# A state-space layer on one core: exp gets PSUM banks of its own, small products share one bank, transposes of a step share a two-bank tile

## Chip, cores, metric

One core of a Trainium2 chip runs the whole program in one launch. The metric is the device time in microseconds (us), the median of the runs; a profiled execution of its own gives the trace. TensorE is called PE, VectorE DVE, ScalarE ACT, GpSimd POOL and SyncE SP in the profile; PEld is PE's weight load.

## The reference, cut to what matters

The network has four residual layers, each `x = x + layer(group_norm(x))`, on x of shape (4, 64, 64, 128). The change touches layer 0 alone, a selective scan over an image in four directions:

```
xz = x @ in_proj.T;  xh, z = split(xz);  z = silu(z)
xc = silu(depthwise_conv3x3(xh) + conv_b)          # 256 channels, 64 x 64
xs = xc along rows, along columns, and both reversed   # 4 directions, L = 4096
x_dbl = einsum(xs, x_proj)                         # splits into dts (8), B (16), C (16)
delta = softplus(dt_proj @ dts + bias)
# per token t, channel d and state n (16 states):
h = exp(delta * A) * h + delta * u * B[n];   y = sum_n h[n] * C[n]
y = sum over the four directions of (y + D * xs), each put back in image order
out = (layer_norm(y) * z) @ out_proj.T
```

Layers 1 to 3 (a Fourier layer, a neural-operator layer, neighbourhood attention) are the same in both kernels.

## The kernel before, in words

**Units and steps.** Layer 0 is cut into 128 units: 4 images (batches), 4 directions in the order k = 1, 3, 0, 2, and 8 chunks of 512 tokens. A unit handles 256 channels as two halves s of 128 partitions. It has 16 steps n, one for each state; four steps make a group g, with q the place in the group. So there are 2048 steps.

**One step** (L405 to L424). POOL multiplies `du` by the broadcast row of B into `dB` (L413, both halves in one instruction). For each half ACT writes `dA = exp(delta * A)` into a PSUM bank (L420) and DVE scans 512 tokens, reading dA from PSUM, dB, and the state so far, into `h` (L421).

**Seven steps behind** (`LAG = 7`) PE turns h round so that the sum over states can be a matmul. `transpose` (L313) transposes four 128 x 128 blocks of h into one PSUM bank `pt` (L318), and ACT copies it to `hT` (L322); a step does this twice, so two banks of `pt` alternate. `products` (L341) multiplies a step's hT by `W` into `yT` (L363). W is C spread out: PE makes `cr` from `xd` (L433), DVE multiplies it by a diagonal mask (L436), four times a unit. After group 3, y is taken from yT (ACT L377 for k=1, else DVE adds at L379) and stored (L384); k=2 also takes statistics (L382).

**The next unit's inputs.** `fetch` (L264) loads u at n=3. `inputs` (L273) makes `xd_ps` on PE (L277) and copies it to `xd` on ACT (L279), writes B to a small DRAM scratch (L281), makes two `dp` on PE (L286), takes Exp twice and one Ln of both halves on ACT (L292, L293), clamps on DVE (L296), and forms `du` on POOL (L299). The scratch is one of three, `B{(8 * k + c) % 3}` (L280). Each group loads its rows of B with a broadcast to 128 partitions, `Bb` (L409), three buffers deep; before the change at the group's own first step.

**Neighbours' pieces.** `before(b)` (L139) is what image b needs ahead of its scan: group norm statistics (`gn_ps`, L148), normalisation (`x_ps` L172, `xn` L173), projection (`xh` L180, copied to `pad` L184), the convolution as nine matmuls a half into `cv` (L193), `zp` (L203), three Silus (L205, L208, L213) with an activation table load on each side, and stores. `after(b)` (L218) is what follows: layer norm (L236), transposes `pg` (L245), an affine copy (L246), the product with z on POOL (L250), `op` (L255), the residual addition (L260). Both are generators: image b+1's before() and image b-1's after() are spread as pieces over the steps of image b, one piece a step but for six values of n, until they are used up. The first image's before() runs ahead of the scans, and the last one's after() behind them.

**What sets the order.** Inside `tc.manual_schedule` (L389) PE, ACT, DVE and POOL run in the order in which the program emits (L386). SP, which issues the DMAs, is not among them: a planner orders its queue. A tile waits for a free buffer of its pool.

**PSUM** has eight banks: `l0ps` 2 (pt), `l0psx` 4, `l0psy` 2 (yT). The four of `l0psx` hold dA and every small product: cr, xd_ps, dp, cv, zp, and those of the pieces.

Of the kernel before, what the change touches and what calls it, by code (L numbers as in the profile page):

```python
# [16 lines left out]
P = 128  # L17
# [64 lines left out]
def layer0(sh, A, x_in, x_out, scr):  # L82
# [4 lines left out]

    tc, nc = sh.tc, sh.nc
    with ExitStack() as ctx:
# [4 lines left out]
        ps = pool("l0ps", 2, space=PSUM)  # L94
        psx = pool("l0psx", 4, space=PSUM)
# [43 lines left out]
        def before(b):  # L139

            st = small.tile([P, NCH, 6], F32, name="gn_st")
            for c in range(NCH):
                t = tmp.tile([P, 4, DM], F32, name="xs", tag="t2", bufs=4)
                nc.sync.dma_start(t, tiles(x_in(b)[c * CH : (c + 1) * CH, :]))
                yield 1
                pt = psx.tile([P, CH], F32, name="gn_ps", tag="x")
                for q in range(4):
                    nc.tensor.transpose(pt[:, q * P : (q + 1) * P], t[:, q, :], sh.ident)  # L148
                nc.vector.bn_stats(st[:, c, :], pt)
            yield 1  # L150
            s_, o_ = sh.group_scale(st, psx, small, "x")
            exp_and_ln()
            yield 1
            for c in range(NCH):
                r0, r1 = max(8 * c - 1, 0), min(8 * c + 9, 64)
# [11 lines left out]
                yield 1  # L167
                for j in range(0, j1 - j0, 3):
                    e = min(j + 3, j1 - j0)
                    pt = psx.tile([P, CH], F32, name="x_ps", tag="x")  # L170
                    for q in range(j, e):
                        nc.tensor.transpose(pt[:, (q - j) * P : (q - j + 1) * P], t[:, q, :], sh.ident)  # L172
                    nc.vector.tensor_scalar(xn[:, j * P : e * P], pt[:, 0 : (e - j) * P], s_, o_, ALU.mult, ALU.add)  # L173
                    yield 1
                for s in range(2):
                    for r in range(r0, r1, 5):
                        n = min(5, r1 - r)
                        pm = psx.tile([P, CH], F32, name="xh", tag="x")
                        o = (r - 2 * j0) * 64
                        nc.tensor.matmul(  # L180
                            pm[:, 0 : 64 * n], lhsT=w_in[:, s, :], rhs=xn[:, o : o + 64 * n], start=True, stop=True
                        )
                        p0 = r - 8 * c + 1
                        nc.scalar.copy(  # L184
                            pad[:, s, p0 : p0 + n, 1:65], pm[:, 0 : 64 * n].rearrange("p (h w) -> p h w", w=64)
                        )
                    yield 1
                o = (8 * c - 2 * j0) * 64
                for s in range(2):
                    pm = psx.tile([P, CH], F32, name="cv", tag="x")  # L190
                    for t in range(9):
                        dy, dx = divmod(t, 3)
# [7 lines left out]
                        if t < 8:  # L200
                            yield 1
# [14 lines left out]
                    yield 1  # L216

        def after(b, st):  # L218

            mv = small.tile([P, NJ, 2], F32, name="ln_mv")  # L220
            for j in range(NJ):
                nc.vector.bn_aggr(mv[:, j, :], st[:, j])
                if j % 8 == 7:
                    yield 1
            rs = sh.rstd(small, mv[:, :, 1], [P, NJ], "ln_r")
            exp_and_ln()
            for c in range(NCH):
                rows = slice(c * CH, (c + 1) * CH)
# [4 lines left out]
                yield 1  # L233
                for q in range(4):
                    j = 4 * c + q
# [3 lines left out]
                    if q % 2:  # L239
                        yield 1  # L240
                yg = tmp.tile([P, 2, CH], F32, name="yg", bufs=1)
                for s in range(2):
                    pt = psx.tile([P, CH], F32, name="pg", tag="x")
# [3 lines left out]
                    yield 1  # L247
# [3 lines left out]
                yield 1  # L251
                op = psx.tile([P, 4, DM], F32, name="op", tag="x")
                for q in range(4):
# [4 lines left out]
                    if q == 1:  # L258
                        yield 1
                nc.vector.tensor_tensor(xr, xr, op, ALU.add)  # L260
                nc.sync.dma_start(tiles(x_out(b)[rows, :]), xr)
                yield 1
# [10 lines left out]
        def inputs(k, c, u):  # L273

            xd_ps = psx.tile([40, CH], F32, name="xd_ps", tag="x")
# [6 lines left out]
            yield  # L282
            dps = []
            for s in range(2):
                dp = psx.tile([P, CH], F32, name="dp", tag="x")
                nc.tensor.matmul(dp, lhsT=w_dt[:, k, s * P : (s + 1) * P], rhs=xd, start=True, stop=True)  # L286
                dps.append(dp)
                yield
            delta = tmp.tile([P, 2, CH], F32, name="delta")

            for s in range(2):
                nc.scalar.activation(delta[:, s, :], dps[s], AF.Exp)  # L292
            nc.scalar.activation(delta, delta, AF.Ln, bias=1.0)  # L293
            yield
            for s in range(2):
                nc.vector.scalar_tensor_tensor(delta[:, s, :], delta[:, s, :], 88.0, dps[s], ALU.min, ALU.max)  # L296
            yield
            du = tmp.tile([P, 2, CH], F32, name="du")
            nc.gpsimd.tensor_tensor(du, delta, u, ALU.mult)  # L299
            yield xd, bd, delta, du  # L300

        for _ in before(0):
            pass
# [3 lines left out]
        for ready in inputs(*units[0][1:], v):  # L307
            pass
# [4 lines left out]
        def transpose(G, q, e):  # L313
            pt = ps.tile([P, 2, 2, P], F32, name="pt")
            for r in range(2):
                t0 = q * P + (2 * e + r) * 32
                for s in range(2):
                    nc.tensor.transpose(  # L318
                        pt[:, r, s, :], G["h"][:, s, t0 : t0 + 32, :].rearrange("p t n -> p (t n)"), sh.ident
                    )  # L320
            hT = tmp.tile([P, 2, 2 * P], F32, name="hT", bufs=4)
            nc.scalar.copy(hT, pt.rearrange("p r s d -> p r (s d)"))  # L322
            return hT

        def transposed(G):
# [3 lines left out]
            if G is not None:  # L329
                q = G["q"]  # L330
                G["q"] += 1
                hTs = [transpose(G, q, 0)]
                copied = G, q, hTs
            yield
            if todo is not None:
                products(*todo)
            if G is not None:
                hTs.append(transpose(G, q, 1))
            yield

        def products(G, q, hTs):  # L341
# [19 lines left out]
            for j in range(4):  # L361
# [4 lines left out]
                    rhs=hTs[j // 2][:, j % 2, :],  # L366
# [20 lines left out]
        pieces = []  # L387
        ends = {}
        with tc.manual_schedule(engines=order):  # L389
            for i, (b, k, c) in enumerate(units):  # L390
                if i % per == 0:
                    ln_st = small.tile([P, NJ, 1, 6], F32, name="ln_st")
                    if b + 1 < NB:
                        pieces.append(before(b + 1))
# [3 lines left out]
                xd, bd, delta, du = ready  # L398
# [5 lines left out]
                coming = None  # L404
                for n in range(NS):  # L405
                    g, q = divmod(n, 4)
                    if q == 0:
                        Bb = tmp.tile([P, 4, CH], F32, name="Bb", bufs=3)
                        nc.sync.dma_start(Bb, bd[4 * g : 4 * g + 4, :].partition_broadcast(P))  # L409
# [3 lines left out]
                    nc.gpsimd.tensor_tensor(dB, du, Bb[:, q : q + 1, :].to_broadcast([P, 2, CH]), ALU.mult)  # L413
                    behind = iter(())
                    if NS * i + n >= LAG:
                        H = queue[0]
                        behind = transposed(H)
                    for s in range(2):
# [5 lines left out]
                        next(behind, None)  # L424
# [3 lines left out]
                    if queue and queue[0]["q"] == 4:  # L428
                        queue.pop(0)
                    if n in (1, 5, 11, 13):  # L430
                        crg = (1, 5, 11, 13).index(n)
                        cr = psx.tile([P, CH], F32, name="cr", tag="x")
                        nc.tensor.matmul(cr, lhsT=sel[:, crg, :], rhs=xd[0:40, :], start=True, stop=True)  # L433
                    if n in (2, 6, 12, 14):
                        W = tmp.tile([P, 16, 32], F32, name="W", bufs=3)
                        nc.vector.tensor_tensor(  # L436
                            W,
                            cr.rearrange("p (a t) -> p a t", t=32),
                            diag[:, int(rev) : int(rev) + 1, :].to_broadcast([P, 16, 32]),
                            ALU.mult,  # L440
                        )
                        Ws[crg] = W
# [11 lines left out]
                    if i + 1 < len(units):  # L454
                        if n == 3:
                            u_next, v_next = fetch(*units[i + 1])
                        if n in (7, 8, 9):
                            coming = coming or inputs(*units[i + 1][1:], v_next)
                            next(coming)
                        if n in (10, 11):  # L460
# [13 lines left out]
                    if n not in (1, 5, 8, 9, 11, 13) and pieces:  # L474
                        if next(pieces[0], None) is None:
                            pieces.pop(0)
                if i + 1 < len(units):
                    u = u_next
                if i % per == per - 1:
                    for p in pieces:  # L480
                        for _ in p:
                            pass
                    pieces = []
                    pieces.append(late(after(b, ln_st)))
            while queue:
                for _ in transposed(queue[0]):
                    pass
                if queue[0]["q"] == 4:
                    queue.pop(0)
            for _ in transposed(None):  # L490
                pass
            for p in pieces:
                for _ in p:
                    pass


def late(pieces, n=8):

    for _ in range(n):
        yield 1  # L500
    yield from pieces
# [1214 lines left out]
```

## Time and profile before

| what | value |
|---|---|
| median of 3 runs | 9484.72 us (9472.2 to 9485.25) |
| the profiled execution, its own time | 9466.91 us |
| its span | 9465.1 us |
| mean granted TensorE clock | 0.889 |
| first scan to last scan of layer 0 | 218.6 to 6968.7 us |
| busy: PE, DVE, ACT, POOL | 7878.8, 7035.5, 6403.3, 5610.1 us |
| scans L421 | 4096, 4998.3 us |
| dB products L413 | 2048, 4829.1 us |
| exponentials L420 | 4096, 2864.3 us |
| copies L322 | 4096, 2416.9 us |

The profile comes from one execution. Busy time is a sum over stages with different limits, so it is read by stage. An idle time stands in front of an instruction and is put down to what ended it. A group's line gives the line of the kernel, engine, operation, tile written and tiles read, shapes and count, then busy time, mean of one in nanoseconds, idle time before it and what ended most of that.

### The profile page before, as it was taken

How to read it: one execution, taken by the hardware profiler on the slowest of the kernel's cores; microseconds unless marked ns; L12 is line 12 of the kernel's file. 1: busy time of each engine (PE TensorE's matmuls, PEld its weight loads, DVE VectorE, ACT ScalarE, POOL GpSimd, SP SyncE). 2: the span in 40 equal slices, each digit the busy share in tenths (PEclk: the TensorE clock that was granted, in tenths of full speed). 3: DMA queues.
4: the chain of work that ended last, by engine and by line, in shares of the span. 5: the costliest groups of instructions: out<-in, count | busy, mean ns of one | idle time of the engine just before them, and what ended most of it. 6: DMA issues, size and time to landing. Idle time of an engine off the chain costs nothing. (4 is left out here: it accounts for less than half of the span.)

```text
span 9465.1 us, 144952 instructions
## 1 busy us (share of the span) xinstructions
PE 7878.8 (83%) x54256; PEld 4499.6 (48%) x54256; DVE 7035.5 (74%) x8298; ACT 6403.3 (68%) x11773; POOL 5610.1 (59%) x2998
## 2 busy tenths in 40 slices
PE   7888888888888888888888888888869967677588
PEld 3444444444444444444444444444447756365366
DVE  1778788898887788888777898998954553443578
ACT  2878787777787777778777777888842211614467
POOL 1777778877777777777777878888840001010133
PEclk8989998888898998889999898999979988778699
DMA  6334443333444443334434333333332124131333
GB/s 112 110 115 127 115 128 123 113 121 128 125 126 118 117 122 115 136 121 119 118 118 126 110 137 123 130 128 114 131 116 53 35 59 132 51 103 50 88 87 86
DMA packets 1148677, 1038.13 MB, mean 110 GB/s; under 512 B 564127, under 2 KB 1001979, under 8 KB 1081156
## 3 DMA queue, kind: packets, MB, share of 16 engines
q1 hardware_dynamic: 1146292, 1027.13, 35.7%
q8 instruction: 426, 6.98, 0.3%
q14 instruction: 279, 2.29, 0.1%
q10 hardware_dynamic: 1680, 1.74, 0.1%
HBM read 845.18 MB, written 181.32 MB: 108 GB/s over the span
## 5 line engine op out<-in xcount | busy, mean ns | idle before, releaser
L421 DVE TENSOR_TENSOR_SCAN h<-dA,state,dB 128x512 f32<-128x512 f32 x4096 | 4998.3, 1271 | 1003.1 <-ACT dA L420 786.5
L413 POOL TENSOR_TENSOR dB<-du,Bb 128x1024 f32<-128x1024 f32 x2048 | 4829.1, 2374 | 1413.6 <-DVE h L421 1146.7
L420 ACT ACTIVATE dA<-delta,A_neg 128x512 f32<-128x512 f32 x4096 | 2864.3, 699 | 505.2 <-DVE h L421 428.5
L318 PEld LDWEIGHTS pt<-ident,h 128*128 128x128 f32 x16384 | 1948.6, 150 | 2008.3 <-issue 1303.5
L318 PE MATMUL pt<-ident,h 128*128 128x128 f32 x16384 | 2756.7, 299 | 103.8 <-ACT hT L322 103.8
L322 ACT COPY hT<-pt 128x512 f32<-128x512 f32 x4096 | 2416.9, 590 | 588.5 <-PE pt L318 552.9
L363 PE MATMUL yT<-hT,W 128*32 128x256 f32 x16384 | 1660.3, 418 | 18.0 <-ACT hT L322 15.2
L433 PE MATMUL cr<-xd,sel 40*128 40x512 f32 x1024 | 667.6, 736 | 460.5 <-DVE h L421 456.3
L363 PEld LDWEIGHTS yT<-hT,W 128*32 128x32 f32 x16384 | 409.7, 111 | 576.2 <-issue 374.0
L193 PE MATMUL cv<-pad,taps 128*128 128x512 f32 x1152 | 608.2, 629 | 0.0
L433 PEld LDWEIGHTS cr<-xd,sel 40*128 40x128 f32 x1024 | 169.4, 207 | 565.8 <-DVE h L421 514.4
L785 POOL TENSOR_TENSOR xg<-xg,so 128x1024 f32<-128x1024 f32 x8 | 26.6, 3343 | 693.4 <-ACT so L785 672.3
L1434 POOL TENSOR_TENSOR S<-S,sm 128x784 f32<-128x784 f32 x128 | 191.1, 1493 | 408.7 <-DVE sm L1432 348.4
L277 PE MATMUL xd_ps<-u,w_x 128*40 128x512 f32 x512 | 281.5, 678 | 134.2 <-DVE h L421 106.1
L286 PE MATMUL dp<-xd,w_dt 65*128 65x512 f32 x512 | 282.2, 634 | 113.6 <-DVE h L421 112.8
L299 POOL TENSOR_TENSOR du<-delta,u 128x1024 f32<-128x1024 f32 x128 | 304.0, 2375 | 66.3 <-DVE delta L296 66.3
L436 DVE TENSOR_TENSOR W<-cr,diag 128x512 f32<-128x512 f32 x512 | 341.4, 667 | 0.0
L785 POOL TENSOR_TENSOR z<-z,sp 128x1024 f32<-128x1024 f32 x16 | 41.8, 2616 | 465.4 <-ACT z L785 465.1
L1441 ACT ACTIVATE S<-S,mx 128x196 f32<-128x196 f32 x512 | 227.9, 448 | 33.9 <-DVE mx L1468 33.4
L785 PE MATMUL pz<-PT,WX 128*68 128x64 f32 x2048 | 167.1, 248 | 100.0 <-DVE WX L785 81.4
L193 PEld LDWEIGHTS cv<-pad,taps 128*128 128x128 f32 x1152 | 197.1, 203 | 106.1 <-issue 99.4
L279 ACT COPY xd<-xd_ps 40x512 f32<-40x512 f32 x128 | 74.3, 580 | 223.2 <-PE xd_ps L277 223.2
(333 smaller groups left out, 7785.7 us busy)
## 6 DMA issues: line engine op xcount, KB each, us to landing
Bb<-l_B SPq DMA_DIRECT2D x512, 1024.0 KB
l_y<-y SPq DMA_DIRECT2D x128, 512.0 KB
wr<-wt SPq DMA_DIRECT2D x256, 136.0 KB
u<-l_xw SPq DMA_DIRECT2D x64, 512.0 KB
y<-l_y SPq DMA_DIRECT2D x64, 512.0 KB
u<-l_xr SPq DMA_DIRECT2D x64, 512.0 KB
V<-l_v SPq DMA_DIRECT2D x512, 49.0 KB
l_xr<-xo SPq DMA_DIRECT2D x64, 256.0 KB
```

The source lines that it names most:

```text
L193: nc.tensor.matmul(pm, lhsT=taps[:, s, t, :], rhs=pad[:, s, dy : dy + 8, dx : dx + 64], start=(t == 0), stop=(t == 8),)
L277: nc.tensor.matmul(xd_ps, lhsT=w_x[:, s, k, :], rhs=u[:, s, :], start=(s == 0), stop=(s == 1))
L286: nc.tensor.matmul(dp, lhsT=w_dt[:, k, s * P : (s + 1) * P], rhs=xd, start=True, stop=True)
L299: nc.gpsimd.tensor_tensor(du, delta, u, ALU.mult)
L318: nc.tensor.transpose(pt[:, r, s, :], G["h"][:, s, t0 : t0 + 32, :].rearrange("p t n -> p (t n)"), sh.ident)
L322: nc.scalar.copy(hT, pt.rearrange("p r s d -> p r (s d)"))
L363: nc.tensor.matmul(U["yT"][e][32 * jo : 32 * jo + 32, qo % 2, :], lhsT=U["Ws"][G["g"]][:, 4 * q + j, :], rhs=hTs[j // 2][:, j % 2, :], sta ...
L413: nc.gpsimd.tensor_tensor(dB, du, Bb[:, q : q + 1, :].to_broadcast([P, 2, CH]), ALU.mult)
L420: nc.scalar.activation(dA, delta[:, s, :], AF.Exp, scale=A_neg[:, k, s, n : n + 1])
L421: nc.vector.tensor_tensor_scan(h[:, s, :, q], dA, dB[:, s, :], state[:, s, n : n + 1], ALU.mult, ALU.add)
L433: nc.tensor.matmul(cr, lhsT=sel[:, crg, :], rhs=xd[0:40, :], start=True, stop=True)
L436: nc.vector.tensor_tensor(W, cr.rearrange("p (a t) -> p a t", t=32), diag[:, int(rev) : int(rev) + 1, :].to_broadcast([P, 16, 32]), ALU.mult,)
```

## The change

1. PSUM pools: `l0ps` has one tile of two banks, `l0psx` three banks, and a new pool `l0psm` one. dA and zp stay in l0psx. cr, xd_ps, dp and all products of the pieces take the one bank of l0psm, `spare`; only the first image's before(), ahead of the scans, takes turns over all four.
2. A step's eight transposes go to one tile `pt` of two banks and are copied by one instruction of 1024 elements a partition. The order within a step becomes: both exponentials and scans, then eight transposes, then the products of the step before, then the copy.
3. cr is made at n = 2, 4, 6, 12 instead of 1, 5, 11, 13, and W is formed after the first scan of the next step. W has four buffers.
4. `inputs` is cut otherwise: dp, its Exp, its Ln and its clamp run half by half, at n = 8 to 11, since the halves share a bank.
5. Bb is asked for a group ahead.
6. Pieces carry a kind: "f" (no PSUM) may run at any step, "m" (takes the spare bank) only outside n = 2, 4, 6 to 12 and outside a running convolution, "c" (three taps of a convolution) starts at n = 14 only and then runs in consecutive steps. A class `Side` paces them: 121 pieces of before() over 29 units, 52 of after() over 22 units.

The diff, cut to its core:

```diff
-        ps = pool("l0ps", 2, space=PSUM)
-        psx = pool("l0psx", 4, space=PSUM)
+        ps = pool("l0ps", 1, space=PSUM)
+        psx = pool("l0psx", 3, space=PSUM)
+        psm = pool("l0psm", 1, space=PSUM)
...
-                    pm = psx.tile([P, CH], F32, name="cv", tag="x")
                     for t in range(9):
+                        if t % 3 == 0:
+                            yield "c"
+                        if t == 0:
+                            pm = bank("cv")
...
-                        if t < 8:
-                            yield 1
...
-            dps = []
+            delta = tmp.tile([P, 2, CH], F32, name="delta")
             for s in range(2):
-                dp = psx.tile([P, CH], F32, name="dp", tag="x")
+                dp = spare("dp")
                 nc.tensor.matmul(dp, lhsT=w_dt[:, k, s * P : (s + 1) * P], rhs=xd, start=True, stop=True)
-                dps.append(dp)
+                nc.scalar.activation(delta[:, s, :], dp, AF.Exp)
+                nc.scalar.activation(delta[:, s, :], delta[:, s, :], AF.Ln, bias=1.0)
                 yield
-            for s in range(2):
-                nc.scalar.activation(delta[:, s, :], dps[s], AF.Exp)
-            nc.scalar.activation(delta, delta, AF.Ln, bias=1.0)
-            yield
-            for s in range(2):
-                nc.vector.scalar_tensor_tensor(delta[:, s, :], delta[:, s, :], 88.0, dps[s], ALU.min, ALU.max)
-            yield
+                nc.vector.scalar_tensor_tensor(delta[:, s, :], delta[:, s, :], 88.0, dp, ALU.min, ALU.max)
+                yield
...
+        spare = lambda name: psm.tile([P, CH], F32, name=name, tag="m")
...
-        def transposed(G):
+        def transposed():
             nonlocal copied
             todo, copied = copied, None
-            if G is not None:
+            pt = None
+            if queue:
+                G = queue[0]
                 q = G["q"]
                 G["q"] += 1
-                hTs = [transpose(G, q, 0)]
-                copied = G, q, hTs
-            yield
+                pt = ps.tile([P, 4, 2, P], F32, name="pt")
+                for j in range(4):
+                    t0 = q * P + j * 32
+                    for s in range(2):
+                        nc.tensor.transpose(
+                            pt[:, j, s, :], G["h"][:, s, t0 : t0 + 32, :].rearrange("p t n -> p (t n)"), sh.ident
+                        )
...
             if todo is not None:
                 products(*todo)
-            if G is not None:
-                hTs.append(transpose(G, q, 1))
-            yield
+            if pt is not None:
+                hT = tmp.tile([P, 4, 2 * P], F32, name="hT")
+                copied = G, q, hT
+                return lambda: nc.scalar.copy(hT, pt.rearrange("p j s d -> p j (s d)"))
+            return lambda: None
...
+        CRS = {2: 0, 4: 1, 6: 2, 12: 3}
+        BUSY = (*CRS, 7, 8, 9, 10, 11)
...
                     if q == 0:
-                        Bb = tmp.tile([P, 4, CH], F32, name="Bb", bufs=3)
-                        nc.sync.dma_start(Bb, bd[4 * g : 4 * g + 4, :].partition_broadcast(P))
+                        B_now = Bb
+                        if g < 3:
+                            Bb = broadcast(bd, g + 1)
+                        elif i + 1 < len(units):
+                            Bb = broadcast(bd_next, 0)
...
-                        next(behind, None)
+                        if s == 0 and cr is not None:
+                            W = Ws[cr[0]] = tmp.tile([P, 16, 32], F32, name="W", bufs=4)
+                            nc.vector.tensor_tensor(W, cr[1]..., diag..., ALU.mult)
+                            cr = None
+                    copy = transposed() if NS * i + n >= LAG else (lambda: None)
+                    copy()
...
+                    if n in CRS:
+                        cr = CRS[n], spare("cr")
+                        nc.tensor.matmul(cr[1], lhsT=sel[:, cr[0], :], rhs=xd[0:40, :], start=True, stop=True)
...
-                        if n in (7, 8, 9):
-                            coming = coming or inputs(*units[i + 1][1:], v_next)
-                            next(coming)
-                        if n in (10, 11):
+                        if n == 7:
+                            coming = inputs(*units[i + 1][1:], v_next)
+                            xd_next, bd_next = next(coming)
+                        if n in (8, 9, 10, 11):
                             next(coming)
...
-                    if n not in (1, 5, 8, 9, 11, 13) and pieces:
-                        if next(pieces[0], None) is None:
-                            pieces.pop(0)
+                    holds = any(d.need == "c" and d.inside for d in sides)
+                    for d in sides:
+                        if d.need == "f" or (d.need == "m" and n not in BUSY and not holds):
+                            ok = d.due(NS * i + n)
+                        else:
+                            ok = d.need == "c" and (d.inside or (n == 14 and d.due(NS * i + n)))
+                        if ok:
+                            d.step()
+                            break
```

`Side` counts the pieces done; `due` is true while `done * slots <= (slot - first) * count`, and `inside` while a convolution has run one or two of its three pieces.

## The prediction

> **What bounds the kernel now.** I read the page's shares first, then the groups, then the waits, then windows batch by batch, then timelines of single steps. The shares say little alone, because layer 0 is three quarters of the span; its groups say more.
>
> ```profile
> PE 7878.8 (83%) x54256; PEld 4499.6 (48%) x54256; DVE 7035.5 (74%) x8298; ACT 6403.3 (68%) x11773; POOL 5610.1 (59%) x2998
> ...
> L421 DVE TENSOR_TENSOR_SCAN h<-dA,state,dB 128x512 f32<-128x512 f32 x4096 | 4998.3, 1271 | 1003.1 <-ACT dA L420 786.5
> L413 POOL TENSOR_TENSOR dB<-du,Bb 128x1024 f32<-128x1024 f32 x2048 | 4829.1, 2374 | 1413.6 <-DVE h L421 1146.7
> L420 ACT ACTIVATE dA<-delta,A_neg 128x512 f32<-128x512 f32 x4096 | 2864.3, 699 | 505.2 <-DVE h L421 428.5
> ```
>
> A step is two scans. In the timeline of an undisturbed stretch scans start 1.175 us apart, so 2.35 us a step; POOL's one product per step takes 2.37. The scans are the chain, and 1003 us of idle VectorE stand before them. The waits name two causes (columns: total, times, longest).
>
> ```profile
> DVE h L421 <- ACT dA L420: 786.5, 721, 6.4
> DVE h L421 <- POOL dB L413: 139.9, 40, 11.5
> ...
> POOL dB L413 <- DMA Bb<-l_B: 145.5, 11, 15.5
> ```
>
> Late exponentials are the large one. Eleven late broadcasts are the other: one at each of the eleven changes of direction 1 to 3, 0 to 2 and 2 to 1, where the last unit of one direction and the first of the next use the same scratch B (15 and 24, 7 and 16, 23 and 8 agree modulo 3; 31 and 0 do not). Windows put prices on neighbours' pieces: batches 0, 1 and 3, then rows k=1 and k=3 of batch 3 (columns: length, busy PE, PEld, DVE, ACT, POOL, clock, DMA, GB/s).
>
> ```profile
> 218.60:1908.40 1689.80, 1461.04 (x9196) 742.34 (x9197) 1404.05 (x1321) 1351.91 (x2294) 1298.12 (x679) 0.90 0.38 119
> 1908.40:3658.40 1750.00, 1499.43 (x9492) 774.30 (x9491) 1454.57 (x1400) 1373.01 (x2327) 1316.12 (x687) 0.90 0.39 122
> ...
> 5414.00:6968.50 1554.50, 1352.04 (x9017) 700.09 (x9016) 1422.35 (x1368) 1271.15 (x2206) 1306.71 (x665) 0.92 0.35 123
> 5414.00:5847.00 433.00, 356.31 (x2371) 190.85 (x2370) 385.52 (x385) 335.36 (x578) 342.57 (x174) 0.90 0.37 128
> 5847.00:6204.90 357.90, 321.97 (x2179) 163.55 (x2178) 340.46 (x320) 312.64 (x547) 323.31 (x166) 0.95 0.36 129
> ```
>
> The k=3 row carries no pieces: 44.7 us a unit, VectorE 42.6 of it. The k=1 row carries after(2): 75 more, about 11 of it its late broadcast, so after() costs 64 a batch. Batch 1 is 195 over batch 3, 9 of that one more late broadcast, so before() costs some 185. From the first scans of neighbouring units the eleven late broadcasts lengthen their units by 7 to 15 us, 120 together. Check: 4 x 1469 clean + 3 x 185 + 3 x 64 + 120 + 8 at the start = 6751, and the scans run from 218.6 to 6968.7.
>
> Two timelines show how ScalarE is late: a convolution's end (ScalarE, then VectorE), and delta's exponentials (same).
>
> ```profile
> 3017.50 1.28 ACT L205 ACT_TABLE_LOAD   x1
> 3018.80 0.69 ACT L205 ACTIVATE xo<-cv,cols 128x512 f32<-128x512 f32 x1
> 3019.38 0.68 ACT L208 ACTIVATE xw<-cv,cols 128x512 f32<-128x512 f32 x1
> 3019.95 0.59 ACT L213 ACTIVATE z<-zp 128x512 f32<-128x512 f32 x1
> 3020.56 1.28 ACT L117 ACT_TABLE_LOAD   x1
> ...
> 3022.65 4.81 DVE L421 TENSOR_TENSOR_SCAN h<-dA,state,dB 128x512 f32<-128x512 f32 x4 [3.83 <-ACT dA L420]
> ```
>
> ```profile
> 5918.85 1.08 ACT L292 ACTIVATE delta<-dp 128x512 f32<-128x512 f32 x2
> 5919.97 1.06 ACT L293 ACTIVATE delta<-delta 128x1024 f32<-128x1024 f32 x1
> ...
> 5921.71 2.46 DVE L421 TENSOR_TENSOR_SCAN h<-dA,state,dB 128x512 f32<-128x512 f32 x2 [1.65 <-ACT dA L420]
> ```
>
> **What the Trainium skill says.** "ScalarE: Activation LUTs", section What ACT_TABLE_LOAD costs, prices an ACTIVATE with immediates at 186 ns + 0.833 ns an element, back-to-back ones overlapping by 93. That is 613 for 512, where the trace has 590, and 1039 for the new copy of 1024; the trace's Ln of 1024 takes 1057. "TensorE: Matmul & The Clock Gate", section What's actually happening, has a half clock after an idle window of about 3.4 us. The trace agrees: after 3.0 us of idle, four transposes take 1.12 us instead of 0.66. "PSUM — Partial Sum Buffer", section Engine vs sequencer instructions: the other compute engines run strictly in order, and matmuls complete in order. I use that below: whatever waits on PE or ScalarE holds back all behind it.
>
> **The transposes and their copy.** Per step the two copies become one. ScalarE saves one fixed part only: two copies are spaced 0.477 each in the timeline; the new one is 0.477 + 512 x 0.833 = 0.90, so 0.05 a step. With two exponentials at 0.62 the step is 2.14 us of ScalarE, under 2.35. The price is the single tile pt: transposes of the next step wait for the whole copy. The drain after the last scan shows the sizes.
>
> ```profile
> 6967.91 1.09 PE L318 MATMUL pt<-ident,h 128*128 128x128 f32 x8
> 6968.66 1.07 ACT L322 COPY hT<-pt 128x512 f32<-128x512 f32 x2 [0.88 <-PE pt L318]
> ```
>
> Eight transposes 1.09, handover 0.09, copy 1.04 (estimate from that page), handover 0.05: 2.27 a step, 0.08 under the scans. The exponentials lie beside the transposes. Cover is thin; at half clock it is gone. Between 0 and +0.15 a step; I take 0.
>
> **Three banks for exp, one for the rest.** In the old order cr, xd_ps, two dp and a whole convolution take banks from exp: cr's matmul waited 456 us for one. Now exp waits for exp alone (and zp). But one bank makes PE wait on VectorE. Worst is n=7: xd_ps waits for W, which now stands between two scans; behind it are 1.95 us of matmul, the copy to xd (0.58) and the next exp (0.70), 3.26 with handovers. VectorE has one scan and mostly one addition left, 1.2 to 1.8: idle 1.5 to 2.0. Delta's burst is split: at n=8 and 10 one Exp and one Ln, 1.11 of pitch plus some 0.4 for dp, against a lead of 1.08 that three banks give (the next dA is ready 2.44 after its bank's release and needed at 3.53). As no lead is left after n=7, I take 0.9 and 0.74. Sum 3.1 to 3.7 a unit. In clean units before, idle VectorE is 3.0, 1.9, 4.2, 3.4 for k=1,3,0,2, mean 3.1. Net 0; bounds -1 and +1 a unit, 128 us either way. Exp/Ln in halves cost ScalarE 0.14 a unit, in that figure. The new order of W, the wider hT and W's fourth buffer change no busy time: 0.
>
> **before().** Its 16 convolutions a batch start at n=14 only, three taps a step: six matmuls at 0.43 are 2.6 us on PE behind transposes and products, 4.0 a step against 2.35. I followed one from n=13. The first two such steps are covered by the exponentials already issued and W's 0.6 us. At n=0 ScalarE ends its copy 0.5 us after the last dA is used up, loads a table while the last taps run, and comes to the next exp after 1.9 for three Silus and 1.28 for the table: VectorE idle 6.3. PE then idles 3 us and starts at half clock: 0.6 more. 7 to 7.5 each, 116 a batch. The 32 xh pieces put a pad copy (0.43) before the next exp, at n=3, 5 and 13 behind W: 0.8 each, 25. Statistics and normalisation are 8 x 0.69 + 16 x 0.65 = 16 us of VectorE, of which I charge 11. 152 against 185: -33 x 3 = -99. Bounds: 5 and 10 us a convolution.
>
> **after().** 32 tensor_scalars at 1.28 in the loop (1.106 over all, the last 32 unshared at 0.41) stay 41 us of VectorE wherever they stand; xr 5.5, aggregates 2; yg's 16 copies behind pg some 6. 55 against 64: -27 in all. Bounds -25 and +15 a batch.
>
> **Broadcasts.** Each Bb is asked for four steps earlier. At a shared scratch only g=3 now follows the next unit's write at n=7: the write, and 5 us until the broadcast lands (asked for at 5814.2, POOL went on at 5819.4), end about n=10, needed at 12. SP's own queue is ordered by the planner, so the y store and the loads that it passes may move; moved, they cost the issue times, 0.3 to 0.6. I leave 1 us each: -109. Bounds 0 and -120.
>
> **Rest.** The last after() runs on one bank: 10.25 us a chunk plus about 0.8, and 7 drain steps at 2.27 for 1.94: +8. First broadcast earlier: -5. The remaining layers: 0, they follow in time. Half-clock steps beside D_diag and k=1's y copies: +5.
>
> Sum: 0 - 99 - 27 - 109 + 8 - 5 + 5 = -227. The profiled execution took 9466.9 (span 9465.1), 17.8 under the median of 9484.7: 9240 there, **9258** for the median.
>
> **Rivals.** First, slower: the pt chain becomes the bound. Half-clock transposes take 1.89 for eight (a timeline shows it at 5926 us), chain 3.07, 0.72 over a scan step. The gain above is used up at 0.11 a step over 2048 steps, or 315 such steps, one in seven. At 0.15 a step it gives +307 - 227: 9565. For it: one tile where there were two, PE waits inside the chain. Against: 2.27 and a full clock in clean stretches. Second, SP's planner keeps the late order and sharing a bank saves no time on pieces: -30 left, 9455. For it: the convolution's burst is untouched. Third, exp's own banks hide more, 4.5 us a convolution (2.7 x 48) and 0.5 us less idle a unit: -130 - 65 more, 9063; against it, W's waits at n=3, 5, 7, 13. That the copy is not one instruction is excluded by the source.
>
> **Numbers.** 0.2% is about what a measurement can tell from no change. Main case 0.58 (9120 to 9400); third 0.12; second 0.16, a quarter of it within 0.2%; slower 0.14. So faster 0.82, same 0.04, slower 0.14; range 9070 to 9450.
>
> **What would show it.** Copy 2048 times at 1.03 to 1.06; waits for Bb from 145 to under 20; PE cr waits under 100; at n=8 a VectorE idle of 1.5 to 2; at n=0 of convolution units one of 5 to 7; batch 1 near 1680. Clean steps at 2.5 or more would make me wrong to the slow side, convolution units under 50 us to the fast side.

## The result, and the profile after

The changed kernel takes 9636.19 us (median of 4 runs, 9630.83 to 9643.28), the kernel before 9484.72. The ratio of the means is 1.0163, 95% interval 1.0146 to 1.0181: slower by 1.6%, clear of the noise, where the prediction had 9258 and faster. The profiled execution has a span of 9641.5 us and a mean clock of 0.901.

Four groups of the page (line, operation, shapes, count, then busy time, mean of one, idle time before it and what ended most of that):

```profile
L432 DVE TENSOR_TENSOR_SCAN h<-dA,state,dB 128x512 f32<-128x512 f32 x4096 | 4987.7, 1267 | 1121.1 <-ACT dA L431 1047.0
...
L338 PE MATMUL pt<-ident,h 128*128 128x128 f32 x16384 | 2399.1, 293 | 1060.0 <-ACT hT L348 1051.0
...
L431 ACT ACTIVATE dA<-delta,A_neg 128x512 f32<-128x512 f32 x4096 | 2694.5, 686 | 210.2 <-DVE h L432 194.1
L348 ACT COPY hT<-pt 128x1024 f32<-128x1024 f32 x2048 | 2070.1, 1011 | 682.6 <-PE pt L338 664.9
```

The new copy is there, 2048 times at 1.01 us. The scans are as busy as before, and the idle time before them has grown from 1003 to 1121 us. In the waits (total, times, longest) no broadcast of B is left, and three others have grown:

```profile
DVE h L432 <- ACT dA L431: 1047.0, 584, 7.2
...
ACT xd L280 <- PE xd_ps L278: 380.2, 128, 15.0
...
PE xd_ps L278 <- DVE W L437: 225.1, 124, 5.3
...
ACT delta L289 <- PE dp L287: 189.2, 173, 3.4
```

Exp is late for 1047 us, where it was 787. The wait of xd for its matmul grew from 223, that of xd_ps for W from 14, and ScalarE's wait for dp from 2. The windows of batches 1 and 3 answer to those of before (length, then busy PE, PEld, DVE, ACT, POOL):

```profile
1961.50:3739.90 1778.40, 1419.04 (x9493) 766.67 (x9492) 1449.88 (x1400) 1331.67 (x1847) 1317.66 (x687) 0.92 0.41 120
...
5511.40:7131.30 1619.90, 1234.40 (x9028) 676.50 (x9025) 1434.38 (x1368) 1247.60 (x1726) 1308.09 (x665) 0.92 0.34 118
```

Batch 1 is 28 us longer than it was, batch 3, which runs no before() beside it, 65. Idle VectorE rose by 33 us in batch 1 and by 53 in batch 3; the other 12 there are VectorE's own work, told of under after() below. I summed the idle time by the step n of a unit over all 128 units. Means in us a unit, of the steps that matter here:

| | n=1 | n=8 | n=9 | n=10 | n=11 | n=12 | n=13 | n=14 | all n, total |
|---|---|---|---|---|---|---|---|---|---|
| before | 0.18 | 1.38 | 0.08 | 0.56 | 2.50 | 0.99 | 0.62 | 0.20 | 1018 |
| after | 2.72 | 1.67 | 1.22 | 0.00 | 1.43 | 0.00 | 0.30 | 0.67 | 1186 |

n=1 is the end of a convolution. 2.72 x 128 / 48 is 7.3 us for each, as predicted (7 to 7.5; its list of signs puts it a step earlier, at n=0). Its timeline in the changed kernel, ScalarE and then VectorE:

```profile
4839.33 1.28 ACT L209 ACT_TABLE_LOAD   x1
4841.59 0.69 ACT L209 ACTIVATE xo<-cv,cols 128x512 f32<-128x512 f32 x1 [0.97 <-PE cv L199]
...
4843.36 1.28 ACT L119 ACT_TABLE_LOAD   x1
...
4845.45 4.81 DVE L432 TENSOR_TENSOR_SCAN h<-dA,state,dB 128x512 f32<-128x512 f32 x4 [7.21 <-ACT dA L431]
```

n=8 is the wait for xd_ps, also as predicted. It reads as a chain in the timeline of one unit of direction 0: the matmul waits for W, the copy to xd for the matmul, the scan for the exp behind the copy.

```profile
6445.24 1.91 PE L278 MATMUL xd_ps<-u,w_x 128*40 128x512 f32 x4 [1.11 <-DVE W L437]
...
6447.18 0.58 ACT L280 COPY xd<-xd_ps 40x512 f32<-40x512 f32 x1 [2.52 <-PE xd_ps L278]
...
6448.46 2.46 DVE L432 TENSOR_TENSOR_SCAN h<-dA,state,dB 128x512 f32<-128x512 f32 x2 [1.51 <-ACT dA L431]
```

n=9 and n=11 are the waits behind Exp and Ln of the two halves. The second one in the same unit:

```profile
6457.88 1.53 PE L287 MATMUL dp<-xd,w_dt 65*128 65x512 f32 x2
...
6459.44 0.60 ACT L289 ACTIVATE delta<-dp 128x512 f32<-128x512 f32 x1 [3.07 <-PE dp L287]
...
6461.38 2.46 DVE L432 TENSOR_TENSOR_SCAN h<-dA,state,dB 128x512 f32<-128x512 f32 x2 [3.25 <-ACT dA L431]
```

ScalarE reaches Exp when its copy is done and stands still for 3.07 us, because dp is the last thing on PE in that step, behind eight transposes, eight matmuls of D_diag and the products. PE had waited 2.10 us for hT itself, and the trace has its granted clock at half from 6455.31 to 6458.72: dp takes 1.53 here and 1.13 at n=8.

### The profile page after: what moved, and what is told of

It reads as the page before. It is cut to its first block, busy times and chain, and to the rows that moved or that the text cites. A ratio compares the mean times of both kernels' runs of the same rounds, so it can differ in the third digit from the quotient of the medians.

```text
span 9641.5 us, 141336 instructions
## 1 busy us (share of the span) xinstructions
PE 7510.1 (78%) x54256; PEld 4450.6 (46%) x54256; DVE 7024.7 (73%) x8298; ACT 6278.3 (65%) x9869; POOL 5615.3 (58%) x2998
## 5 line engine op out<-in xcount | busy, mean ns | idle before, releaser
L338 PE MATMUL pt<-ident,h 128*128 128x128 f32 x16384 | 2399.1, 293 | 1060.0 <-ACT hT L348 1051.0
L431 ACT ACTIVATE dA<-delta,A_neg 128x512 f32<-128x512 f32 x4096 | 2694.5, 686 | 210.2 <-DVE h L432 194.1
L348 ACT COPY hT<-pt 128x1024 f32<-128x1024 f32 x2048 | 2070.1, 1011 | 682.6 <-PE pt L338 664.9
L373 PE MATMUL yT<-hT,W 128*32 128x256 f32 x16384 | 1411.7, 419 | 0.6 <-ACT hT L348 0.6
L199 PE MATMUL cv<-pad,taps 128*128 128x512 f32 x1152 | 537.3, 606 | 0.3
L373 PEld LDWEIGHTS yT<-hT,W 128*32 128x32 f32 x16384 | 332.9, 111 | 376.4 <-issue 361.1
L280 ACT COPY xd<-xd_ps 40x512 f32<-40x512 f32 x128 | 74.4, 581 | 380.2 <-PE xd_ps L278 380.2
L287 PE MATMUL dp<-xd,w_dt 65*128 65x512 f32 x512 | 307.1, 683 | 12.7 <-DVE delta L292 12.0
L289 ACT ACTIVATE delta<-dp 128x512 f32<-128x512 f32 x256 | 153.2, 598 | 189.6 <-PE dp L287 189.2
```

Of the source, the lines that this page charges most:

```text
L199: nc.tensor.matmul(pm, lhsT=taps[:, s, t, :], rhs=pad[:, s, dy : dy + 8, dx : dx + 64], start=(t == 0), stop=(t == 8),)
L338: nc.tensor.transpose(pt[:, j, s, :], G["h"][:, s, t0 : t0 + 32, :].rearrange("p t n -> p (t n)"), sh.ident)
L348: return lambda: nc.scalar.copy(hT, pt.rearrange("p j s d -> p j (s d)"))
L373: nc.tensor.matmul(U["yT"][e][32 * jo : 32 * jo + 32, qo % 2, :], lhsT=U["Ws"][G["g"]][:, 4 * q + j, :], rhs=hT[:, j, :], start=((e, jo) n ...
L431: nc.scalar.activation(dA, delta[:, s, :], AF.Exp, scale=A_neg[:, k, s, n : n + 1])
```

## The experiments

Each was timed in three rounds. The kernel before measured 9473 to 9477 us beside them. The expectations weigh three theories of the loss: 1, the waits around the one bank for small products; 2, the chain of one tile of transposes and one copy; 3, the pieces spread thin over an image.

**Two parts alone, on the kernel before.** First the tile of transposes (`ps` one tile of two banks, `transposed` as in the changed kernel, called after both scans); nothing else.

> The kernel before with one part of the change alone: the two-bank tile of transposes and its one copy per step, ahead of the rest; PSUM pools, inputs, broadcasts and pieces as before. Theory 1 (the loss of the whole change comes from the one bank for small products): this part costs nothing, -80 to +30 us against before, since pure scan steps of the changed kernel still run at 2.35 us. Theory 2 (the chain of one tile and one copy is the loss): +130 us or more.

9389.5 us, ratio 0.991 (0.9889 to 0.9932): 88 us faster, just beyond what theory 1 allowed. In the kernel before, the chain of one tile and one copy is no loss. Nor is it the loss in the changed one: two edits below leave it as it is and together take 410 us off. So theory 2 and the first rival are out. The part gains more than the 0 that the prediction took.

Then the broadcasts:

```diff
-    Bb = tmp.tile(...); nc.sync.dma_start(Bb, bd[4 * g : 4 * g + 4, :].partition_broadcast(P))
+    B_now = Bb
+    Bb = broadcast(bd, g + 1) if g < 3 else broadcast(bd_next, 0)
```

> The kernel before with the broadcasts of B asked for a group ahead, nothing else. All theories: -90 to -120 us, the eleven late broadcasts gone (145 us of waits to under 20), as the prediction priced them. If it is under -40, the gain seen at the changes of direction in the changed kernel came from something else, for example the planner's order of the y store.

9375.96, ratio 0.9898 (0.9877 to 0.9919): 101 us faster. The prediction had 109 for this. The waits of POOL for Bb, 145.5 before:

```profile
POOL dB L425 <- DMA Bb<-l_B: 20.4, 7, 5.8
```

**Two edits of the changed kernel.** In the first, Exp and Ln of a half run a step behind their dp:

```diff
                 nc.tensor.matmul(dp, ...)
+                yield
                 nc.scalar.activation(delta[:, s, :], dp, AF.Exp)
                 nc.scalar.activation(delta[:, s, :], delta[:, s, :], AF.Ln, bias=1.0)
-                yield
                 nc.vector.scalar_tensor_tensor(delta[:, s, :], ...)
                 yield
```

> The changed kernel with Exp and Ln of each half put one step behind their dp matmul (n = 9 and 11 instead of 8 and 10). Theory 1: ScalarE no longer waits for dp (189 us of waits to under 40), idle VectorE before the steps n = 9 to 12 falls by a third or more, -80 to -200 us against the changed kernel's 9636. Theory 2 and theory 3 (the spread pieces are the loss): no change within 30 us.

9314.88, ratio to before 0.9829 (0.9803 to 0.9854): 321 us faster than the changed kernel, from a moved `yield`. That is more than theory 1 had. ScalarE's wait for dp falls from 189.2 to 1.8 us. Two other waits of this run:

```profile
DVE h L431 <- ACT dA L430: 710.7, 329, 7.2
...
ACT xd L280 <- PE xd_ps L278: 394.1, 128, 15.0
```

Idle VectorE at n=9 fell from 1.22 to 0.29 a unit, at n=11 from 1.43 to 0.14, at n=14 from 0.67 to 0.39. The wait for xd stayed. So 187 us less of ScalarE's waits went with 309 us less of VectorE's idle time (1186 to 877 in all). I take the rest to be PE, which was late behind them; that isn't shown.

In the second, W no longer stands between xd_ps and its bank:

```diff
-        CRS = {2: 0, 4: 1, 6: 2, 12: 3}
-        BUSY = (*CRS, 7, 8, 9, 10, 11)
+        CRS = {2: 0, 4: 1, 5: 2, 12: 3}
+        BUSY = (*CRS, 6, 7, 8, 9, 10, 11)
```

> The changed kernel with the third cr at n = 5 instead of 6, so that W is formed at n = 6 and xd_ps at n = 7 finds its bank free (n = 6 is closed to pieces in place of n = 5). Theory 1: waits of xd_ps for W (225 us) fall under 40 and idle VectorE before n = 8 (1.67 us a unit) falls under 0.6, -80 to -150 us against 9636. Theories 2 and 3: within 30 us.

9506.05, ratio to before 1.0031 (1.0019 to 1.0043): 130 us faster than the changed kernel. Idle at n=8 fell from 1.67 to 0.90, less than to the 0.6 expected. The wait of xd fell from 380.2, and some came back at cr, whose wait for W was 12 in the changed kernel:

```profile
PE cr L451 <- DVE W L437: 191.7, 133, 11.7
...
ACT xd L280 <- PE xd_ps L278: 154.8, 128, 14.9
```

**What adds.** The two parts that helped, together on the kernel before; and the two edits together on the changed one.

> The kernel before with two parts of the change: the two-bank tile of transposes with one copy, and the broadcasts a group ahead. If the two add, 9477 - 88 - 101 = 9288 us, within 25. Then all the rest of the change (bank of its own for small products with the inputs cut half by half, W's place, the pieces) costs 348 us together. If the two share a cause, 9340 or more.

9276.04, ratio 0.979 (0.9774 to 0.9806). They add, to within 12 us. So the bank for small products, the re-cut inputs, W's place and the new pieces cost 360 us together.

> The changed kernel with Exp and Ln a step behind their dp and the third cr at n = 5. Theory 1 (all waits around the one bank at n = 7 to 11 are the loss): the two add, 9636 - 321 - 130 = 9185 us, idle VectorE before n = 8 to 12 under 1.5 us a unit. If clearing one only moves the wait to the other (the lead that ScalarE has is what counts), 9250 to 9310.

9225.75, ratio 0.9735 (0.9721 to 0.975). That is 410 us off the changed kernel, of the 451 that the two edits gave apart. It lies between the two expectations (9185; 9250 to 9310), so nearly all adds, and a little of the wait moves. Idle VectorE before n = 8 to 12 is 1.4 us a unit, within theory 1's limit of 1.5. Theory 1 stands: these waits account for more than the 360 us just told. Whether banks of its own for exp gain anything is not shown. This run is 50 us ahead of the one with the shared PSUM just told, but it also takes Exp and Ln of delta in halves, and that alone gains more with the PSUM shared (below).

**The pacing undone.** `due` returns true from `first` on.

> The changed kernel without the pacing: a piece is due as soon as its kind and step allow. Theory 3 (spreading the pieces thin over the image costs, each one breaking ScalarE's lead anew): 9480 to 9580 us. Theory 1: pieces cost what they cost wherever they stand, 9610 to 9670. If spreading helps as intended: above 9680.

9717.75, ratio 1.0258 (1.0241 to 1.0276): 82 us slower than the changed kernel. Spreading the pieces helps; theory 3 is wrong. This run has another use. Its pieces are used up early, so directions 3, 0 and 2 of batch 3 run without any. Windows of these three rows of eight units (columns as above):

```profile
6047.00:6428.40 381.40, 297.40 (x2179) 158.89 (x2176) 341.10 (x319) 308.78 (x427) 322.42 (x166) 0.93 0.33 121
6428.40:6818.10 389.70, 295.45 (x2315) 168.96 (x2313) 341.63 (x322) 309.88 (x426) 322.56 (x166) 0.98 0.35 121
6818.10:7201.80 383.70, 298.14 (x2168) 159.31 (x2168) 351.53 (x346) 303.25 (x418) 318.77 (x162) 0.92 0.30 110
```

The first row took 357.9 before with the same VectorE work, 340.5. An ordinary unit of the changed kernel, one without pieces, has 5.0, 6.0 and 4.0 us of idle VectorE in these rows. The prediction had 3.1 as a mean. By steps the mean of the three rows is 1.60 at n=8, 1.46 at n=9, 1.47 at n=11 and 0.42 at n=14.

**The burst of delta in the shared PSUM.** On the run with the two parts, Exp and Ln of the first half at n=10, of the second at n=11, clamps behind; dp stay two steps ahead, in two banks.

> The kernel before with the two parts that helped (tile of transposes, broadcasts ahead), PSUM shared as before, and delta's burst cut: Exp and Ln of the first half at n = 10, of the second at n = 11, both clamps after that, dp still two steps ahead in two banks. Theory: the idle of 2.6 us before n = 11 is the burst of 2.1 us against a lead near 1 us; cut in two it falls under 1.3 us, -150 us against the run with the two parts, near 9140. If the lead does not come back within a step, the second half costs what the first saved: within 40 us of that run.

9139.04, ratio 0.964 (0.9626 to 0.9655): 137 us faster than without, as expected. But idle before n=11 only fell from 2.59 to 1.87, where under 1.3 was expected; the rest came off n=12 to 14. Then the second half a step further on, and each clamp right behind its Ln (the cut shows the step alone):

```diff
-                        if n in (10, 11):
+                        if n in (10, 12):
                             next(coming)
```

> The run with tile of transposes, broadcasts ahead and delta's burst cut (9139 us), with the second half two steps after the first (n = 12 instead of 11), each clamp right behind its Ln. If ScalarE's lead comes back within those two steps, the idle of 1.87 us before n = 11 falls under 1 and does not return at n = 13: -60 to -120 us, near 9050. If the lead comes back too slowly in pure scan steps (0.08 us a step), within 30 us of 9139.

9013.5, ratio 0.9513 (0.9499 to 0.9527): 126 us more, a little beyond the 60 to 120 expected. Idle before n=11 fell from 1.87 to 0.21; n=10 rose from 0.52 to 1.22, and 11 to 13 hold 1.0 together. Its scans, from the page:

```profile
L424 DVE TENSOR_TENSOR_SCAN h<-dA,state,dB 128x512 f32<-128x512 f32 x4096 | 4942.3, 1265 | 483.5 <-ACT dA L423 335.1
```

**After().** Its pieces cost more in the changed kernel than predicted. I thought of the queue behind W at n=3, 5, 13, and barred pg and op from these steps.

> The changed kernel with after()'s pieces that use the spare bank (two pg, one op a chunk) barred from n = 3, 5 and 13, where they queue behind W on PE and in front of the next exp; they run at n = 0, 1, 14, 15. If that queue is what makes after() dearer than predicted (some 87 us a batch instead of 55): -60 to -130 us against 9636. If after() costs the same wherever it stands: within 30 us.

9715.34, ratio 1.0256 (1.0239 to 1.0273): 79 us slower, against both expectations. Batch 3, with no convolutions, took 1622.7 us against 1619.9, so getting them out of the queue behind W gains nothing. Batches 1 and 2 took 31 to 35 us more; I take it that pieces then had to fit between convolutions. The theory falls.

The other suspect was the layer norm on VectorE. The view of that line in the kernel before (count, then minimum, median and maximum in ns):

```profile
L236 DVE TENSOR_SCALAR yf<-yf,ln_mv,ln_r x128: 381/409/2599, 1971.1 to 7062.2; 128x256 f32<-128x256 f32 x128
```

One shape, 381 to 2599 ns. What stretches it can be read from the trace of that kernel. Here two of them follow each other; the second starts under POOL's product and ends 0.15 us after it (1973.82 against 1973.67):

```profile
1971.07 2.75 DVE L236 TENSOR_SCALAR yf<-yf,ln_mv,ln_r 128x256 f32<-128x256 f32 x2
...
1971.30 2.37 POOL L413 TENSOR_TENSOR dB<-du,Bb 128x1024 f32<-128x1024 f32 x1 [0.28 <-DVE h L421]
```

Of the 96 inside the scans, 53 start while a product of POOL runs, and 51 of these end 0.148 to 0.155 us after it. The edit gives the product to ScalarE (`nmr`, formed once an image, is minus the mean times the scale), on the 9013.5 us run and then on the changed kernel:

```diff
-    nc.vector.tensor_scalar(y[:, q, :], y[:, q, :], mv[:, j, 0:1], rs[:, j : j + 1], ALU.subtract, ALU.mult)
+    nc.scalar.activation(y[:, q, :], y[:, q, :], AF.Identity, scale=rs[:, j : j + 1], bias=nmr[:, j : j + 1])
```

> The run with the second half two steps later (9013.5 us), with after()'s 32 layer norm products a batch moved from VectorE to ScalarE (Identity with scale and bias). On VectorE they take 380 to 2601 ns for the same 128 x 256, mean 1.13 us in that run, 44 us a batch inside the scans. If it is POOL's product that stretches them and they are the larger part of after(): -60 to -110 us. If ScalarE then falls behind instead (0.5 us each before an exp): -30 to +30 us.

8886.97, ratio 0.9384 (0.9368 to 0.9399): 127 us faster again, more than the 60 to 110 expected, and the fastest of all. The product takes 0.59 us on ScalarE. The total of idle VectorE is 605 us as in the run before it (611), so ScalarE did not fall behind.

> The changed kernel with the same one edit: after()'s layer norm products on ScalarE. After() costs some 100 us a batch in the changed kernel, where the prediction had 55. If the layer norm products on VectorE (mean 1.4 us there) are most of it: -100 to -160 us against 9636. If ScalarE's lead, short in this kernel, is what after() breaks, the products on ScalarE break it too: within 60 us of 9636.

9558.62, ratio 1.0087 (1.007 to 1.0104): 78 us faster than the changed kernel, between the two expectations. Batch 3 went from 1619.9 to 1579.4.

## Why the prediction was wrong

**Three banks for exp, one for the rest** is the step that failed: "Net 0; bounds -1 and +1 a unit". The ordinary unit was put at 45.9 us; the piece-free rows of the unspread run give 47.7, 48.7 and 48.0, and one piece-free unit of direction 1 there 46.9, mean 47.8. That is +1.9 x 128 = 243 us, twice the bound. Its term for n=7 was right: idle 1.5 to 2.0 forecast, 1.60 measured in ordinary units (1.67 over all), and the run with the early third cr removes half of it. The term for delta's halves was mis-sized. It had 0.9 and 0.74, from "some 0.4 for dp", and nothing at n=14. Measured in ordinary units are 1.46, 1.47 and 0.42: 1.7 more, some 219 of the 243 us. The run with Exp a step later shows the cause: over all units the idle at n=9, 11 and 14 falls by 2.50 us together, 320 us in all. ScalarE stood still for a matmul issued in the same step. The prediction had one unit's hand timeline at full clock with D_diag left out; in direction 0 of batch 3, with D_diag in front of dp, idle at n=9 and 11 is 1.9 and 2.5.

**The transposes and their copy:** the copy takes 1.01 for the 1.04 assumed, and alone the part is worth 88 us. The prediction had no gain within its bounds. In the kernel before, the second half of a step's transposes stood behind the products; in the run with this part alone idle VectorE in direction 0 of batch 3 fell from 45.2 to 29.5 us over its eight units. Which of order and copy did it was not tried.

**before()** fits as a difference: batches 1 and 2 are 158.5 and 151.6 longer than batch 3, forecast 152, and a convolution costs 7.3. Batch 0, which carries before() and no after(), doesn't fit: it stands 207 us over 32 ordinary units, where 152, and 8 for the start, were forecast. Why is open. **The broadcasts** were right: -101 alone for -109. **The planner** left no late broadcast, so that half of the second rival is out. Its other half, that the shared bank saves no time on pieces, fits: with both kinds of pieces batch 1 stands 248 us over its 32 ordinary units, and before the change it stood 248 over the 1469 of its clean ones (1750.0, less three late broadcasts of 11). The forecast was 207. Spread pieces, which got no price, are worth 82 us.

**after()** was mis-sized: 55 a batch forecast. Batch 3 less 32 ordinary units of 47.8 leaves 90. The layer norm products were put at 41 "wherever they stand", and there the step failed: in batch 3 they take 58 (43 in that batch before; 47 and 45 in batches 1 and 2 of the changed kernel), as more of them start under a product of POOL, 66 of 96 against 53. The mean of 1.28 in the loop was a slip besides: 1.106 over all with 0.41 for the last 32 leaves 1.34. Moving the products took 40 off that batch. The other 14 measure about 31. What makes pg, yg and op so dear is open; taking them out of the queue behind W did not help.

The sum, on the two profiled executions: 9240 forecast, 9643.3 measured, 403 between them (378 between the medians). 243 for ordinary units, 3 x 35 = 105 for after() (batch 3's excess, taken for all three), 3 x 3 for before() as a difference, 6 for the tail (13.7 where 8 was forecast) and 10 for the start (5 us later instead of 5 earlier) make 373. The other 30 are less than the 47 that batch 0 has over its forecast.

The rival on the slow side named the wrong wait. The transposes' chain takes 2.25 a step in the drain after the last scan, where 2.27 was forecast; what cost the time was ScalarE waiting, in order, for a matmul issued in the same step.

## What to carry to other kernels

Where engines run in the order of the program, emit a consumer a step or more after its producer, and measure it: the same Exp right behind its matmul or one step later differed by 321 us here, and a burst cut in two and set two steps apart gained 263 in all. Price a wait at a shared bank by what stands behind the waiting instruction on its engine and on the next one, for every variant of the unit, not for the lightest. And take a change apart: two of its parts gained 200 us together, hidden under a third that lost 360.

## What the runs showed of the hardware

The layer norm product on VectorE, 128 x 256 in SBUF, takes 0.38 us or up to 2.60, by what POOL does at the time. In the kernel before, 51 of the 53 that start under a product of POOL end 0.148 to 0.155 us after it; of the other 43 inside the scans, 40 take 0.38 to 0.41. After the last scan, with POOL mostly idle, four in a row take 1.38. The Trainium skill, "SBUF — State Buffer", section Who interferes with whom, has tensor_scalar among the operations that can take the port pair VectorE shares with GpSimd, where the later one blocks for the whole instruction. The trace agrees: the later one waits for the end of POOL's 2.37 us. The prediction priced these products by their mean and had not seen that they can be moved: on ScalarE they cost no idle time that shows.

The 3.4 us of idle that the prediction quotes for half clock are not needed in these traces: 3.0 led to it in the prediction's own example, and in the unit shown above PE was idle for 2.10 us, did its transposes from 6454.23, and was granted half clock from 6455.31.
